# A GRU with a residual on one core: fewer warm-up products, one load moved, and the operand sums, banks and turns of the first steps rearranged

## The chip, the cores and the metric

The kernel runs on one core of a Trainium2 chip. Its metric is the device time in microseconds (us) of one execution; a lower time is better. Five engines work side by side, each on its own list of instructions in order, and they wait for each other by semaphores: TensorE (PE, matrix products, with the loading of weights shown apart as PEld), VectorE (DVE), ScalarE (ACT), GpSimd (POOL) and SyncE (SP, which here only issues transfers).

## What is computed

A recurrent unit runs over 128 steps for 64 sequences; both the input and the state h have 512 elements. The output is x plus all the new states.

```python
def step(h, inp):
    x_t, prop = inp
    comb = jnp.concatenate([x_t, h], axis=-1)
    z = jax.nn.sigmoid(comb @ Wz + bz)
    r = jax.nn.sigmoid(comb @ Wr + br)
    comb2 = jnp.concatenate([x_t, r * h], axis=-1)
    h_cand = jnp.tanh(comb2 @ Wh + bh)
    h_new = (1.0 - z) * h + z * h_cand
    h_next = jnp.where(prop, jnp.tanh(h_new @ Wp + bp), h_new)
    return (h_next, h_new)
```

`prop` is true in every fourth step but the last. All is in float32. Each weight has 1024 rows: the upper 512 multiply x, the lower 512 multiply h or r*h.

## The kernel before, in words

**Layout.** The 128 partitions hold two halves of the 512 columns for 64 sequences each, so that a state is a tile of 128 x 256. A product (`product`, L203, over `products`, L191) takes a 128-row block k of the transposed state as the stationary side and 256 columns of a weight as the moving side, once for each half. Each of these two matmuls is two records in the trace, so a product is four records and a gate, with its four blocks k, sixteen. The blocks are taken in the order 0, 2, 1, 3 (`ORDER`), and a weight arrives in two transfers, of blocks 0 and 1 and of blocks 2 and 3, so a gate's second product needs the second transfer.

**Turns.** Before h, r*h or x can be the stationary side, it is transposed: `turn` (L212) writes eight small transposes into PSUM, four into each of two banks (`turn_ps[c]`, c = 0 and 1), and DVE or ACT copies them out (L210). The sigmoid of r and the tanh of the candidate are written to another part of the same two banks (`act_ps`), from which DVE reads them.

**The step.** In the loop over t (L674) each step makes the products of r, then of z, the turn of r*h, and the products of the candidate; ACT and DVE make the gates and the new state (tanh L802, times z L803, plus the kept part L808); h is turned for the next step. The x part of each gate with its bias lies ready in `cp` and is copied into the gate's bank before the products (`seed`, L409, on ACT).

**The x part** is independent of the recurrence. Its products stand in a queue, and `fill(n)` (L417) puts n of them between the pieces of a step, so that PE has work while the other engines make the gates. Steps 0 to 3 and the last four use plain products (`plain`, L428). From step 4 on the steps are taken together in a scheme with seven products in place of eight, on two levels: the outer operands are numbered 1 to 7, and so are the inner ones (`batch`, L509, two outer products at a time). It needs sums of blocks of x, made on POOL (`sum_raw12`, `sum_raw34`, `sum_s12` and others), and sums of blocks of the x weights, made once at the start (`sum_outer`, and for each operand i `sum_inner(i, engine)`, three additions, and `sum_inner_1`, one in place). A batch uses four banks, `scratch` q, r, a and x, in which it makes first the products a, r, x, q and then x, q, r. After the first part ACT copies x and q out (L541, L542) and DVE adds (L543, L544, `end_1`); after the second ACT copies q (L549) and DVE adds r, x and q in this order (L550 to L552, `end_2`). Steps 4 to 7 use batches of their own: (1, 0) in step 1, (1, 1) and (1, 2) in step 2. POOL adds their results to the blocks in `cp` (`pair_left`, `pair_right`, L623 and L629).

**The start.** Transfers are issued on SP's queue in the order of the code, over eight semaphores, so that one waits for the landing of the one eight before it. PE makes products of zeros (`idle`, L179) and the turns of x of steps 0 and 1, then the x products of these two steps, the turn of h, and step 0. `turn_x(t)` turns the x of step t; ACT makes its copies from step 2 on. The x of steps 8 and later goes another way (`words_x`, `planes_x`, a transposing transfer, and `join_x`, on ACT).

The order on every engine is the order in which the code is written: nothing rearranges it.

Of the kernel before, what the change touches and what calls it, by code (L numbers as in the profile page):

```python
# [17 lines left out]
def kernel(  # L18
# [29 lines left out]
    nc = tc.nc  # L48
# [9 lines left out]
    FIRST = 2  # L58
    LAST = T // Q4 - 1
    R, Z, H_ = range(3)  # L60
# [74 lines left out]
    for i in range(3):  # L135
        for k in (0, 2):
            load_w(wh[i], gates_in[i][D:, :], k, k + 2, nc.sync)
        if i == 0:
            load_x(xr[0], 2, 2, 2)

    dummy = const.tile([1, 1], F32, name="dummy")
# [37 lines left out]
    def idle(n):  # L179
        for i in range(n):  # L180
            s = i % S
            nc.tensor.matmul(
                (rc, zp)[i // S % 2][s * B : (s + 1) * B, :, :],
                lhsT=zeros[:, :B],
                rhs=zeros,
                start=True,
                stop=True,
            )
# [14 lines left out]
    def product(ps, lT, w, k, start=False):  # L203
        s0, c0 = divmod(k, C)
        products(ps, lT[:, c0, ts(s0, B)], lambda s: w[:, k, ts(s, N)], start)
# [24 lines left out]
    def new_T(tag, name):  # L230
        return two.tile([P, C, P], F32, tag=tag, name=name)
# [7 lines left out]
    def new_xT(g):  # L239
        if g not in xT:  # L240
            xT[g] = xtp.tile([P, Q4, C, P], F32, tag="xT", name=f"xT_{g}")

    def turn_x(t, eng=nc.scalar):
        g, i = divmod(t, Q4)
        new_xT(g)
        src = xr[g] if g < 2 else early[g]
        for c in range(C):
            turn(src[:, i, :], xT[g][:, i], c, f"xT_{t}", eng)
# [79 lines left out]
    def sum_inner(i, eng):  # L328
        eng.tensor_sub(tt[:, i - 1, 1], inner(i, 1, 1), inner(i, 0, 1))
        eng.tensor_add(tt[:, i - 1, 0], tt[:, i - 1, 1], inner(i, 0, 0))  # L330
        eng.tensor_sub(tt[:, i - 1, 2], inner(i, 1, 0), tt[:, i - 1, 0])

    def sum_inner_1(i, eng):
        eng.tensor_sub(inner(i, 0, 1), inner(i, 0, 1), inner(i, 0, 0))  # L334
# [18 lines left out]
    def sum_raw34(g):  # L353
        v = xT[g]
        sx[g, 34] = one.tile([P, 4, C, B], F32, tag="s73", name=f"s34r_{g}")
        four([sx[g, 34][:, n] for n in range(4)], v[:, 2], v[:, 3])
# [6 lines left out]
    def sum_s12(g):  # L363
        v = xT[g]
        o = sx[g, "o12"] = one.tile([P, 2, 2, P], F32, tag="o12", name=f"o12_{g}")
        nc.gpsimd.tensor_add(o[:, 0], v[:, 2:4, 0, :], v[:, 2:4, 1, :])
        nc.gpsimd.tensor_sub(o[:, 1], o[:, 0], v[:, 0:2, 0, :])
        s = sx[g, 56] = one.tile([P, 4, 2, B], F32, tag="s56", name=f"s56_{g}")
        four([s[:, n] for n in range(4)], o[:, :, 0], o[:, :, 1])
# [47 lines left out]
    def fill(n):  # L417
        for _ in range(min(n, len(queue))):
            unit, end = queue.pop(0)
            unit()  # L420
            if end is not None:
                pending.append(end)
# [86 lines left out]
    def batch(n, ms):  # L509

        def region(ps, m):
            return ps[:, m].rearrange("p g u -> p (g u)")

        def unit(ps, m, j, e, start):
            g, i = ms[m]
            a, b = terms(i)[e]
            products(
                region(ps, m),
                lhs(g, a, j),
                lambda s: factor(b, j)[:, s],  # L520
                start and m == 0 and e == 0,
            )

        def units(ps, j, start):
            return [
                lambda m=m, e=e: unit(ps, m, j, e, start)
                for m, (_, i) in enumerate(ms)
                for e in range(len(terms(i)))
            ]

        def blocks():
            return MB[n].rearrange("p m b g (a u) -> p m b a g u", a=2)

        def end_1():
            MB[n] = mbp.tile([P, 2, 2, 3, P], F32, tag="mb", name=f"mb_{ms[0][0]}_{ms[0][1]}")
            for m, (g, i) in enumerate(ms):
                M[g, i] = MB[n][:, m]
            nm = len(ms)
            T2[n] = one.tile([P, 2, 3, P // 2], F32, tag="cx", name=f"cx_{ms[0][0]}_{ms[0][1]}")
            q1 = one.tile([P, 2, 3, P // 2], F32, tag="cq", name=f"cq_{ms[0][0]}_{ms[0][1]}")  # L540
            nc.scalar.copy(T2[n][:, :nm], x_ps[:, :nm])  # L541
            nc.scalar.copy(q1[:, :nm], q_ps[:, :nm])  # L542
            nc.vector.tensor_add(T2[n][:, :nm], r_ps[:, :nm], T2[n][:, :nm])  # L543
            nc.vector.tensor_add(blocks()[:, :nm, 0, 0], a_ps[:, :nm], q1[:, :nm])  # L544

        def end_2():
            q2 = one.tile([P, 2, 3, P // 2], F32, tag="cq", name=f"cq2_{ms[0][0]}_{ms[0][1]}")
            nm = len(ms)
            nc.scalar.copy(q2[:, :nm], q_ps[:, :nm])  # L549
            nc.vector.tensor_add(blocks()[:, :nm, 0, 1], r_ps[:, :nm], q2[:, :nm])  # L550
            nc.vector.tensor_add(blocks()[:, :nm, 1, 0], x_ps[:, :nm], q2[:, :nm])
            nc.vector.tensor_add(blocks()[:, :nm, 1, 1], q_ps[:, :nm], T2[n][:, :nm])  # L552

        free = units(a_ps, 2, True)
        one_ = [units(r_ps, 5, True), units(x_ps, 7, True), units(q_ps, 1, True)]

        one_ = sum(one_ if ms[0][0] >= FIRST else one_[2:] + one_[:2], [])
        two_ = units(x_ps, 4, False) + units(q_ps, 6, False) + units(r_ps, 3, False)
        seq = [(u, None) for u in free + one_ + two_]
        size = sum(len(terms(i)) for _, i in ms)  # L560
        for n_units, end in ((4 * size, end_1), (7 * size, end_2)):
            seq[n_units - 1] = (seq[n_units - 1][0], end)
        return seq
# [59 lines left out]
    def pair_left(a, p1, p2):  # L623
        nc.gpsimd.tensor_add(
            M[1, p2], M[1, p2], bias0.unsqueeze(1).to_broadcast([P, 2, 3, P])
        )
        add(c_block(1, a, 0), m_(1, p1), m_(1, p2))

    def pair_right(a, p1, x_):  # L629
        nc.gpsimd.tensor_add(  # L630
            M[1, x_], M[1, x_], bias[:, 1, 0:3, :].unsqueeze(1).to_broadcast([P, 2, 3, P])
        )
        add(c_block(1, a, 1), m_(1, p1), m_(1, x_))
# [11 lines left out]
    )  # L645


    idle(24)
    turn_x(0, nc.vector)
    idle(8)  # L650
    turn_x(1, nc.vector)
    idle(12)
    nc.gpsimd.tensor_sub(bias_d, bias[:, 1, 0:3, :], bias0)
    h = h_init
    hT = new_T("hT", "hT_init")
# [18 lines left out]
    for t in range(T):  # L674
# [3 lines left out]
        pair, u = divmod(t - 3, 8)  # L678
        even, odd = FIRST + 2 * pair, FIRST + 2 * pair + 1
        here = pair >= 0 and even * Q4 < T  # L680
        places = PLACES[u]
        if t == 0:
            queue.extend(plain(2) + plain(3))
            places = (12, 12)
        elif t == 1:
            queue.extend(batch((1, 0), [(1, 1), (1, 2)]))
            places = (8, 6)
        elif t == 2:
            queue.extend(batch((1, 1), [(1, 10), (1, 11)]) + batch((1, 2), [(1, 8), (1, 9)]))
            places = (12, 8)  # L690
        elif t == 3:
            queue.extend(batches(FIRST))
            places = (8, 8, 6)
# [3 lines left out]
        thin = t >= T - 9  # L697
        if thin:

            places, behind = TAIL[t - (T - 9)]  # L700
# [3 lines left out]
        if t == T - 10:  # L704

            places = (4, 6)
# [16 lines left out]
        for k in ORDER:  # L723
            product(slots[R], hT, wh[R], k)
        if t < 2:
            turn_x((2, 6)[t])
        if t == 1:
            for i in (7, 4):
                sum_inner(i, nc.gpsimd)
                sum_inner_1(i, nc.gpsimd)  # L730
        read_out()
        if t == 2:
            pair_left(0, 1, 2)
        if u == 0 and pair >= 1 and odd - 2 < LAST:
            outer_u2(odd - 2)
        if t == 3:
            sum_s12(FIRST)
        rh = two.tile([P, N], F32, tag="rh", name=f"rh_{t}")
        for c in range(C):
            nc.scalar.activation(act_ps[c], slots[R][:, ts(c, P)], AF.Sigmoid)  # L740
# [9 lines left out]

        for k in ORDER[: 2 if thin else 3]:
            product(slots[Z], hT, wh[Z], k)
        rhT = new_T("rhT", f"rhT_{t}")
        for c in range(C):
            turn(rh, rhT, c, f"rhT_{t}", nc.vector)
# [9 lines left out]
        nc.scalar.activation(slots[Z], slots[Z], AF.Sigmoid, scale=-1.0)  # L765
        nc.vector.tensor_mul(keep, slots[Z], h)
        join(1)
        if t == 1:
            sum_inner(5, nc.vector)
            sum_inner_1(5, nc.vector)  # L770
        seed(Z, t + 1)
        if prop:
            nc.scalar.copy(cut(slot_p), bias[:, :, 3, :])
# [40 lines left out]
            planes_x(3)  # L814
        read_out()
        fill(places[0] if thin else 5 if places[1] > 6 else 4)
        h = h_new
        if not last:
            hT = new_T("hT", f"hT_{t}")
            turn(h, hT, 0, f"hT_{t}", nc.vector)  # L820
            fill(places[1] if thin else 1 if places[1] > 6 else 2)
            turn(h, hT, 1, f"hT_{t}", nc.scalar)
        fill(places[2] if thin else places[1] - 6)
        if t == 0:
            sum_outer_1()
            for i in (1, 2, 3):
# [11 lines left out]
                turn(h, hT, c, f"hpT_{t}", (nc.vector, nc.scalar)[c])  # L838
            fill(behind[1] if thin else 2)
        if t == 0:  # L840
            turn_x(4)
            turn_x(5)
            sum_raw12(1)
        elif t == 1:
            turn_x(7)
            sum_raw34(1)
        elif t == 2:
            pair_right(0, 1, 10)
        elif t == 3:
            pair_left(1, 8, 9)  # L850
            pair_right(1, 8, 11)
# [35 lines left out]
                    outer_c12(odd)  # L887
        if u == 7 and pair >= -1 and (even + 2) * Q4 < T:
            sum_raw12(even + 2)
            if pair >= 0:  # L890
                sum_s12(even + 2)
        if pair >= 0:
            if u in (1, 2):
                for n in range(2):
# [11 lines left out]
        n = 0  # L906
        if t >= T - CHUNK:
            n = {T - 2: 3, T - 1: 1}.get(t, 0)
        elif j == Q4 - 1:
            n = 4  # L910
# [58 lines left out]
```

## Time and profile before

| | us |
|---|---|
| median of 3 runs | 1335.53 |
| lowest and highest | 1335.13 and 1337.05 |
| the profiled execution, its own time | 1334.71 |
| its span | 1332.9 |
| busy in it: PE, PEld | 1322.6, 1115.6 |
| busy in it: DVE, ACT, POOL | 706.6, 635.4, 932.5 |
| mean granted clock of PE | 0.999 |

An execution's own time is a little longer than the span of its trace. The costliest groups are the recurrent products, for instance

```profile
L194 PE MATMUL rc<-wh,rhT 128*64 128x256 f32 x2048 | 246.1, 379 | 0.0
L582 POOL TENSOR_TENSOR cp<-mb,mb 128x768 f32<-128x768 f32 x74 | 134.5, 1817 | 102.4 <-ACT rc L411 54.4
```

A group's line has the line of code, the engine, what is written from what, the number of instructions; then the busy time in us and the mean duration of one in ns; then how long the engine stood idle just before them, and what ended most of that. Matmuls overlap, so one lasts longer (379 ns) than the distance between two starts (0.108 us where sixteen take 1.73 us). In a timeline each row gives the start, the time until the last of the row's instructions ended, the instruction and, in brackets, the idle time before it with the releaser. A line of the waits gives the total, how often, and the longest.

### The profile page before, as it was taken

How to read it: one execution, taken by the hardware profiler on the slowest of the kernel's cores; microseconds unless marked ns; L12 is line 12 of the kernel's file. 1: busy time of each engine (PE TensorE's matmuls, PEld its weight loads, DVE VectorE, ACT ScalarE, POOL GpSimd, SP SyncE). 2: the span in 40 equal slices, each digit the busy share in tenths (PEclk: the TensorE clock that was granted, in tenths of full speed). 3: DMA queues.
4: the chain of work that ended last, by engine and by line, in shares of the span. 5: the costliest groups of instructions: out<-in, count | busy, mean ns of one | idle time of the engine just before them, and what ended most of it. 6: DMA issues, size and time to landing. Idle time of an engine off the chain costs nothing.

```text
span 1332.9 us, 37646 instructions
## 1 busy us (share of the span) xinstructions
PE 1322.6 (99%) x15336; PEld 1115.6 (84%) x15336; DVE 706.6 (53%) x1874; ACT 635.4 (48%) x1860; POOL 932.5 (70%) x1135
## 2 busy tenths in 40 slices
PE   9999999999999999999999999999999999999998
PEld 5788888888888888888888888888888888888765
DVE  3555555555555555555555555555555555555444
ACT  1454455454544544545445454445545444554433
POOL 5687876777777768776787767786777687767400
PEclk9999999999999999999999999999999999999999
DMA  9222233121221222313112221222212222131300
GB/s 293 45 49 49 49 65 64 33 65 39 59 65 33 65 51 47 65 40 81 42 40 58 64 65 33 56 43 65 65 33 65 49 50 65 33 76 38 98 24 17
DMA packets 119277, 77.79 MB, mean 58 GB/s; under 512 B 65984, under 2 KB 114240, under 8 KB 119104
## 3 DMA queue, kind: packets, MB, share of 16 engines
q1 hardware_dynamic: 118352, 74.14, 24.1%
q8 instruction: 121, 1.98, 0.6%
q10 hardware_dynamic: 496, 0.72, 0.2%
q0 software_dynamic: 256, 0.52, 0.1%
q14 instruction: 52, 0.43, 0.1%
HBM read 42.86 MB, written 16.78 MB: 45 GB/s over the span
## 4 chain that ended last, share of the span: by engine, by line
PE 96%; DMA 2%; DVE 1%; POOL 1%; ACT 0%; issue 0%; SPq 0%; DVEq 0%; ACTq 0%; POOLq 0%
PE rc L194 33%; PE zp L194 20%; PE scratch_q L194 11%; PE scratch_r L194 10%; PE scratch_x L194 10%; PE scratch_a L194 6%; PE turn L219 5%; DMA wh<-in_L_cond_Wz_dram 1%; DMA wx<-in_L_cond_Wz_dram 1%; POOL cp L582 0%; POOL mb L630 0%; ACT xT L283 0%; SPq L96 0%; DVE wx L334 0%; DVE tt L330 0%
## 5 line engine op out<-in xcount | busy, mean ns | idle before, releaser
L194 PE MATMUL rc<-wh,rhT 128*64 128x256 f32 x2048 | 246.1, 379 | 0.0
L582 POOL TENSOR_TENSOR cp<-mb,mb 128x768 f32<-128x768 f32 x74 | 134.5, 1817 | 102.4 <-ACT rc L411 54.4
L194 PE MATMUL zp<-wh,hT 128*64 128x256 f32 x1536 | 204.5, 379 | 0.0
L194 PEld LDWEIGHTS rc<-wh,rhT 128*64 128x64 f32 x2048 | 168.9, 137 | 39.9
L194 PE MATMUL rc<-wh,hT 128*64 128x256 f32 x1536 | 186.3, 383 | 0.3
L901 POOL TENSOR_TENSOR xr<-xr,h 128x256 f32<-128x256 f32 x127 | 92.7, 730 | 105.2 <-DVE h L808 105.2
L194 PEld LDWEIGHTS rc<-wh,hT 128*64 128x64 f32 x1536 | 121.6, 137 | 36.2 <-issue 9.8
L582 POOL TENSOR_TENSOR cp<-mb 128x768 f32<-128x768 f32 x46 | 83.6, 1816 | 95.1 <-ACT rc L411 93.7
L194 PEld LDWEIGHTS zp<-wh,hT 128*64 128x64 f32 x1536 | 119.3, 137 | 24.8
L210 DVE COPY rhT<-turn 128x256 uint16<-128x256 uint16 x256 | 97.5, 420 | 79.9 <-PE turn L219 78.8
L803 DVE TENSOR_TENSOR turn<-turn,z 128x128 f32<-128x128 f32 x256 | 75.4, 294 | 120.9 <-ACT turn L802 119.3
L740 ACT ACTIVATE turn<-rc 128x128 f32<-128x128 f32 x256 | 55.3, 260 | 167.3 <-issue 111.6
L210 ACT COPY hT<-turn 128x256 uint16<-128x256 uint16 x127 | 47.3, 373 | 168.6 <-DVE hT L210 130.4
L582 POOL TENSOR_TENSOR mb<-mb,mb 128x768 f32<-128x768 f32 x58 | 105.4, 1817 | 9.5 <-DVE mb L552 9.5
L411 ACT COPY rc<-cp 128x256 f32<-128x256 f32 x256 | 96.4, 376 | 25.9 <-DVE cp L436 14.4
L550 DVE TENSOR_TENSOR mb<-scratch_r,cq 128x384 f32<-128x384 f32 (+1 forms) x105 | 58.4, 556 | 93.2 <-ACT cq L549 93.2
L802 ACT ACTIVATE turn<-rc 128x128 f32<-128x128 f32 x256 | 55.2, 260 | 105.0 <-PE rc L194 103.9
L543 DVE TENSOR_TENSOR cx<-scratch_r,cx 128x384 f32<-128x384 f32 (+1 forms) x105 | 58.3, 556 | 86.2 <-ACT cx L541 86.2
L764 ACT ACTIVATE z<-zp 128x256 f32<-128x256 f32 x128 | 49.2, 384 | 96.2 <-PE zp L194 96.2
L283 ACT COPY xT<-xv 128x512 uint16<-128x512 uint16 x120 | 91.3, 764 | 0.0
L808 DVE TENSOR_TENSOR h<-turn,keep 128x128 f32<-128x128 f32 x254 | 74.0, 291 | 15.2
L219 PEld LDWEIGHTS <-h 128*64 128x64 bf16 x1016 | 68.3, 110 | 14.3 <-DVE h L808 7.9
(163 smaller groups left out, 3026.8 us busy)
## 6 DMA issues: line engine op xcount, KB each, us to landing
xr<-in_x_dram SPq DMA_DIRECT2D x62, 256.0 KB, 4.0
out_dram<-xr SPq DMA_DIRECT2D x62, 256.0 KB, 3.3
xs<-in_x_dram SPq DMA_DIRECT2D x56, 256.0 KB, 4.3
wx<-in_L_cond_Wz_dram SPq DMA_DIRECT2D x2, 512.0 KB, 8.0
wx<-in_L_cond_Wh_dram SPq DMA_DIRECT2D x2, 512.0 KB, 11.4
wh<-in_L_cond_Wr_dram SPq DMA_DIRECT2D x2, 512.0 KB, 13.4
wh<-in_L_cond_Wz_dram SPq DMA_DIRECT2D x2, 512.0 KB, 11.8
wh<-in_L_cond_Wh_dram SPq DMA_DIRECT2D x2, 512.0 KB, 10.9
```

The lines of the kernel that those rows point to most:

```text
L194: nc.tensor.matmul(ps[s * B : (s + 1) * B], lhsT=lhs, rhs=rhs(s), start=start, stop=True, skip_group_check=True,)
L210: (eng.copy if eng is nc.scalar else eng.tensor_copy)(dst, src)
L219: nc.tensor.transpose(pt[s * B : (s + 1) * B, w, :], words.rearrange("p (n w) -> p w n", w=2)[:, w, :], ident16,)
L283: nc.scalar.copy(xT[g][:, i].bitcast(U16).rearrange("p c (n w) -> p w c n", w=2), xv[g][:, i])
L411: nc.scalar.copy(cut(slots[i]), G[t][:, :, i, :])
L543: nc.vector.tensor_add(T2[n][:, :nm], r_ps[:, :nm], T2[n][:, :nm])
L550: nc.vector.tensor_add(blocks()[:, :nm, 0, 1], r_ps[:, :nm], q2[:, :nm])
L582: nc.gpsimd.tensor_add(dst, a, b)
L740: nc.scalar.activation(act_ps[c], slots[R][:, ts(c, P)], AF.Sigmoid)
L803: nc.vector.tensor_mul(pc, pc, z[:, ts(c, P)])
L808: nc.vector.tensor_add(h_new[:, ts(c, P)], pc, keep[:, ts(c, P)])
L901: nc.gpsimd.tensor_add(xr[g][:, j, :], xr[g][:, j, :], h_new)
```

## The change

The change touches only the start and steps 0 to 3.

- 44 products of zeros become 28: 16 before the turn of x of step 0, 4 before that of step 1, 8 after it.
- The x of steps 2 and 3 is loaded behind the recurrent weights of z instead of in front of them.
- The turn of x of step 2 goes from behind r's products of step 0 to behind the first three of z's.
- The turn of x of step 4 goes from the end of step 0 to the middle of the last six x products there; that of step 5 stays at the end.
- The turn of x of step 7, and the sums of x of steps 6 and 7, go from the end of step 1 to in front of h's turn.
- The sums of operand 5 go from DVE to POOL, in front of those of operand 7; those of operand 4 go from step 1 to step 2.
- The batch (1, 2) makes its products in the order a, r, x, q, as the later ones do; (1, 0) and (1, 1) keep a, q, r, x.
- On POOL `pair_right(0, 1, 10)` goes behind the sums of x of steps 8 to 11, and the second set of these sums from step 3 to the end of step 2.

```diff
-        if i == 0:
+        if i == Z:
             load_x(xr[0], 2, 2, 2)
...
-        one_ = sum(one_ if ms[0][0] >= FIRST else one_[2:] + one_[:2], [])
+        one_ = sum(one_[2:] + one_[:2] if n in ((1, 0), (1, 1)) else one_, [])
...
-    idle(24)
+    idle(16)
     turn_x(0, nc.vector)
+    idle(4)
+    turn_x(1, nc.vector)
     idle(8)
-    turn_x(1, nc.vector)
-    idle(12)
...
         if t < 2:
-            turn_x((2, 6)[t])
+            if t:
+                turn_x(6)
         if t == 1:
-            for i in (7, 4):
+            for i in (5, 7):
                 sum_inner(i, nc.gpsimd)
                 sum_inner_1(i, nc.gpsimd)
         read_out()
         if t == 2:
             pair_left(0, 1, 2)
+            sum_inner(4, nc.gpsimd)
+            sum_inner_1(4, nc.gpsimd)
...
-        if t == 3:
-            sum_s12(FIRST)
...
         for k in ORDER[: 2 if thin else 3]:
             product(slots[Z], hT, wh[Z], k)
+        if t == 0:
+            turn_x(2)
         rhT = new_T("rhT", f"rhT_{t}")
...
-        if t == 1:
-            sum_inner(5, nc.vector)
-            sum_inner_1(5, nc.vector)
...
         fill(places[0] if thin else 5 if places[1] > 6 else 4)
+        if t == 1:
+            turn_x(7)
+            sum_raw34(1)
         h = h_new
         if not last:
             hT = new_T("hT", f"hT_{t}")
             turn(h, hT, 0, f"hT_{t}", nc.vector)
             fill(places[1] if thin else 1 if places[1] > 6 else 2)
             turn(h, hT, 1, f"hT_{t}", nc.scalar)
-        fill(places[2] if thin else places[1] - 6)
+        if t == 0:
+            fill(3)
+            turn_x(4)
+            fill(3)
+        else:
+            fill(places[2] if thin else places[1] - 6)
...
         if t == 0:
-            turn_x(4)
             turn_x(5)
             sum_raw12(1)
-        elif t == 1:
-            turn_x(7)
-            sum_raw34(1)
-        elif t == 2:
-            pair_right(0, 1, 10)
...
             sum_raw12(even + 2)
-            if pair >= 0:
-                sum_s12(even + 2)
+            sum_s12(even + 2)
+        if t == 2:
+            pair_right(0, 1, 10)
```

## The prediction

> **What bounds the kernel now.** I read the profile page first, for the engine that carries the span. In these lines of it the reader is to see that TensorE (PE) is busy 99% of the span and that the chain that ended last lies 96% on it, so an edit pays only where it removes time in which PE stands still, or work from PE itself.
>
> ```profile
> PE 1322.6 (99%) x15336; PEld 1115.6 (84%) x15336; DVE 706.6 (53%) x1874; ACT 635.4 (48%) x1860; POOL 932.5 (70%) x1135
> PE 96%; DMA 2%; DVE 1%; POOL 1%; ACT 0%; issue 0%; SPq 0%; DVEq 0%; ACTq 0%; POOLq 0%
> ```
>
> Next, the waits of PE over the first 130 us. The whole run adds hardly any (its largest sum, 1.6, is the 1.4 below and one more), so all that waits can still give is 3.6 us, and the wait for the first zeros, which the change leaves.
>
> ```profile
> PE turn L219 <- DVE h L808: 1.4, 1, 1.4
> PE rc L182 <- DVE zeros L73: 1.2, 1, 1.2
> PE zp L194 <- DMA wh<-in_L_cond_Wz_dram: 0.7, 1, 0.7
> PE scratch_q L194 <- DVE mb L552: 0.5, 1, 0.5
> PE turn L219 <- ACT hT L210: 0.4, 1, 0.4
> PE turn L219 <- ACT xT L210: 0.4, 1, 0.4
> PE scratch_r L194 <- POOL s L344: 0.2, 1, 0.2
> ```
>
> Third, PE's timeline of the start (first column: start, us). The reader is to see two rates, 0.43 us for two zero products up to 7.17 and 0.21 after it, then x products without a gap, and at 23.41 the wait for the second half of z's recurrent weights.
>
> ```profile
> 6.75 0.62 PE L182 MATMUL rc<-zeros 128*64 128x512 bf16 x2
> 7.17 0.40 PE L182 MATMUL zp<-zeros 128*64 128x512 bf16 x2
> 7.42 0.38 PE L182 MATMUL rc<-zeros 128*64 128x512 bf16 x2
> ...
> 9.37 1.89 PE L194 MATMUL scratch_q<-wx,xT 128*64 128x256 f32 x16
> ...
> 23.41 1.08 PE L194 MATMUL zp<-wh,hT_init 128*64 128x256 f32 x8 [0.69 <-DMA wh<-in_L_cond_Wz_dram]
> 24.32 0.39 PE L219 MATMUL turn<-ident,rh 128*64 128x128 bf16 x8
> 24.55 0.60 PE L194 MATMUL zp<-wh,hT_init 128*64 128x256 f32 x4
> ```
>
> Last, VectorE (DVE) in step 1: the four sums of operand 5 hold it from 43.95 to 48.25, and h, done at 49.79, comes after them.
>
> ```profile
> 43.95 0.55 DVE L329 TENSOR_TENSOR tt<-wx 128x384 f32<-128x384 f32 x1
> 44.53 1.24 DVE L330 TENSOR_TENSOR tt<-tt,wx 128x384 f32<-128x384 f32 x1
> 45.80 1.25 DVE L331 TENSOR_TENSOR tt<-wx,tt 128x384 f32<-128x384 f32 x1
> 46.97 1.36 DVE L334 TENSOR_TENSOR wx<-wx 128x384 f32<-128x384 f32 x1
> 48.25 0.54 DVE L543 TENSOR_TENSOR cx<-scratch_r,cx 128x384 f32<-128x384 f32 x1
> ```
>
> I sum against the profiled execution: span 1332.9, its own time 1334.71, which is 0.82 under the median of the runs, 1335.53. A measurement of this kernel tells about 0.2% (2.7 us) from no change.
>
> **Fewer zeros.** 44 zero products become 28: 16 x 0.21 = 3.4 us at the slow rate. With two turns at 0.43 each, PE is done with them at 1.20 + 3.42 + 0.43 + 0.85 + 0.43 = 6.33, plus eight zeros across the change of rate, 7.6, instead of 9.37. But then the weights rule. The trace's landings (the last of a transfer's 16 parts): x weights of r 7.88, of z 9.20 and 12.16, of h 14.50 and 15.83; recurrent r 17.67 and 19.78; x of steps 2 and 3 20.50 and 20.89; recurrent z 22.03 and 23.37. A product takes 0.43, and the second product of each gate needs the second half. So, after the change: first product 7.92; z's second waits for 12.16; the recurrent r's second, ready at 19.34, waits for 19.78; all of r is done at 21.1.
>
> Here a rule speaks against the cut. The row: the rate doubles at 7.2, 6.0 us after PE's first product. The Trainium skill ("TensorE: Matmul & The Clock Gate", What's actually happening) says that the clock is doubled only after a busy window of about 3.4 us, and that the windows run free of the kernel. To be sure to hold one whole window, PE must be busy for two, 6.83 us. The cut leaves 28 x 0.2135 + 2 x 0.43 = 6.84 at the slow rate, from 1.20 to 8.04: just enough. By the row nothing is lost, by the rule's worst phase 0.1 us; I take nothing. The opposite fear, that the new pauses for weights halve the clock again, has a row too: between 48.2 and 51.6 PE stands still for 1.35 + 0.36 us, and the gate that starts at 51.50 still takes 1.73 us.
>
> **x of steps 2 and 3 behind z's weights.** These two transfers take 20.89 - 19.78 = 1.11 us of the stream. Without them in front, z's halves land at 20.9 and 22.26, and x at 22.98 and 23.37, the same total. On SyncE's queue the four transfers swap places: z's go out at 6.43 and 7.89, x at 9.56 and 12.17, over ten us before it lands, so the issue is not late. PE: first z product at 21.1, second waits to 22.30, two products to 23.16. There the turn of x of step 2 now stands, and waits for 23.37: 23.42. The turn of r*h behind it writes the same two banks, so it waits for ScalarE's (ACT) copies out of them. The trace has this pair: two turns one after the other at 37.52 took 1.14 us until the next product instead of 0.44. So the last z product comes at 23.42 + 1.14 = 24.56, as before 24.55. ACT has room (1.80 us idle before z). I take +0.1; bounds -0.5 (x lands with z) and +0.5 (x 0.4 later). The zeros are hidden by the same landing: with all 44, PE would have reached z's second product at 22.50.
>
> **Turns of steps 4 and 5 apart.** That same pair, 1.14 us before step 1, is split: the first goes between six x products (0.43 each, three after), so its copies end before the second. 0.44 remain: -0.70. Bounds -0.75 and -0.5. The in-place sums behind it on DVE come 0.2 later and end at about 40.1, 0.7 before they would hold up r*h.
>
> **Operand 5's sums to GpSimd (POOL), step 1's turn of step 7 ahead of h's.** DVE is free, so (in the clock of before) the first copies end at 46.92 and 47.31 on ACT, L543 runs at 47.0, L544 at 47.45, then h's halves end at 48.51 and 49.04. The changed program's instruction order shows that the turn of step 7 waits for DVE, which reads the same banks until h is done: its halves come at 48.57 and 49.10. h's first turn waits for ACT's copy of step 7, which starts 0.33 after the first transpose and takes 0.37: 49.33. Then 0.11, two r units 0.65, 0.11: step 2 starts at 50.20 instead of 51.50, -1.30. Bounds: -1.7 (both stalls wholly gone, 1.35 + 0.36) and -0.9 (each of the four handovers 0.1 longer).
>
> POOL pays with time that is covered. One operand's four sums take 4 x 1.05 = 4.2 there (L329 to L329, 15.99 to 19.12 for three). Operand 5 is done at 46.0, 7 at 50.2, the sums of steps 6 and 7 at 51.9; PE wants the latter at 55.2. Operand 4 moves behind step 1's additions to xr and to the left blocks, ends at 60.5, and is first needed several batches later. If this cover were gone, PE would wait for the rest one for one.
>
> **The order of step 2.** The third batch of step 2 waited 0.74 us start to start (66.65 to 67.39) as its q bank is read last by DVE. Taking r first starts at 66.65, since r is read by 66.4 and x by 66.9. But then h's turn, at 67.62, meets h, which ends at 67.93: 67.98, one unit, the other half at 68.53, two units, step 3 at 69.29 instead of 69.62: -0.3, not -0.74. Bounds -0.5 and -0.1.
>
> **pair_right behind the sums of steps 8 to 11.** Those sums (5.1 us) start when ACT has joined xT, 63.1, and end at 68.2; pair_right's two additions (3.7) end at 71.9. ACT's seed of step 4, 70.5 in this clock, waits for that, and behind it on ACT the copy of q (L549), 1.5 late at 72.8; DVE wants it at 74.0, after r*h. Covered by 1.2. The wait at 76.28 stays: there DVE's L550 stands behind r*h's copies, in both kernels. From step 4 on nothing differs.
>
> **Sum.** +0.1 - 0.7 - 1.3 - 0.3 = -2.2: 1332.5 for the profiled execution, and with 0.82 a median of 1333.3, -0.17%.
>
> **Rivals.** (a) The start gains too. If transfers run faster than in this profile, before is held by its PE work (gapless from 9.37, only 0.69 behind the weights) and after by the weights: -0.5 to -1.4 more, 1331.9 to 1332.8. For it: 0.69 is little; against: 332 to 350 GB/s in this stretch, all engines full. 25%. (b) The change does less than it says: x lands 0.5 late and the new handovers in shared banks take back half of step 1: -0.8 to -1.5, 1334.0 to 1334.7. 10%. (c) Slower, by the clock alone: the cut of the zeros leaves no whole busy window in an unlucky phase, and pauses then break each later one. Half rate costs half of the PE time that it covers; the pauses for weights hide 0.4 + 0.5 + 0.7 = 1.6 of that, and 2.2 is gained elsewhere. To lose 2.7, half rate must last 13 us, to about 21; to 24.6 it costs some 7: 1340. Against it stands the kept rate at 51.50. 4%. The likeliest case has 61%.
>
> **How the numbers follow.** The likeliest case by itself runs from 1332.7 to 1333.9, by the bounds of step 1 and x's landing. Eight in ten: from the middle of (a) less 0.7 for the runs' own scatter (1335.13 to 1337.05) to the end of (b) and as much, 1331.6 to 1335.2. Faster by over 0.2% means under 1332.86: all of (a) and a ninth of the likeliest, 32%. Slower: (c) and a bad draw, 5%. Within: 63%.
>
> **What would show it.** Right: the first x product at 7.9; a PE wait of about 0.75 for z's weights near 22.3 and of 0.25 for x near 23.4; r*h's turn waiting for ACT's xT; step 1 starting 0.6 earlier, step 2 1.9, step 3 2.2 earlier; waits of PE for h of 0.3 at step 2's end. Wrong: z's last start product clearly before 24.1 or after 25.0, zero products at 0.21 instead of 0.11 or gates at 3.5 instead of 1.73 after 8.1, or a PE wait for POOL between 50 and 75.

## The result and the profile after

| | before | after |
|---|---|---|
| median of 20 runs each, us | 1335.75 (1335.06 to 1337.48) | 1333.75 (1332.85 to 1335.46) |
| profiled execution: own time, span | 1334.71, 1332.9 | 1334.15, 1332.3 |

The ratio is 0.9985, with a 95% interval of 0.9979 to 0.9991: 2.0 us faster, 0.15%. The forecast was 1333.3, within 0.2%. The two profiled executions differ by only 0.56 us, because that of before lay 1.04 under its median and that of after 0.40 above. So the shares below are taken from differences inside one trace, and only then set against the medians.

The engine line and the chain of the page say the same as before: TensorE carries the span.

```profile
PE 1321.7 (99%) x15320; PEld 1110.8 (83%) x15320; DVE 702.6 (53%) x1870; ACT 635.4 (48%) x1860; POOL 934.9 (70%) x1139
PE 96%; DMA 2%; DVE 1%; ACT 1%; issue 0%; SPq 0%; DVEq 0%; ACTq 0%
```

PE's waits in the first 130 us (the columns are the sum in us, the number of waits, the longest):

```profile
PE zp L194 <- DMA wh<-in_L_cond_Wz_dram: 1.4, 2, 1.1
...
PE turn L219 <- DVE h L808: 0.4, 2, 0.2
...
PE turn L219 <- ACT xT L210: 0.3, 1, 0.3
...
PE scratch_r L194 <- DVE mb L550: 0.2, 1, 0.2
PE turn L219 <- DMA xr<-in_x_dram: 0.2, 1, 0.2
```

The wait of 1.4 for h is now 0.4 in two pieces, the waits for DVE's read of the q bank (0.5) and for hT (0.4) are gone, and the weights of z cost 1.4 instead of 0.7. The wait of 0.2 for POOL's sums in before is the one for L550 here: it stands ahead of the same product of step 3 (76.28 in before, 75.65 in after, 0.22 both times), and only the releaser that the list names has changed. In after POOL's sums are done at 68.9, so this wait is not for them.

PE's timeline of the start (the first column is the start in us):

```profile
7.82 1.95 PE L194 MATMUL scratch_q<-wx,xT 128*64 128x256 f32 x16 [0.36 <-DMA wx<-in_L_cond_Wr_dram]
...
23.73 1.08 PE L194 MATMUL zp<-wh,hT_init 128*64 128x256 f32 x8 [1.13 <-DMA wh<-in_L_cond_Wz_dram]
24.98 0.42 PE L219 MATMUL turn<-ident,xr 128*64 128x128 bf16 x8 [0.17 <-DMA xr<-in_x_dram]
25.75 0.58 PE L219 MATMUL turn<-ident,rh 128*64 128x128 bf16 x8 [0.35 <-ACT xT L210]
26.13 0.63 PE L194 MATMUL zp<-wh,hT_init 128*64 128x256 f32 x4
```

The cut of the zeros brings the first x product from 9.37 to 7.82, and nothing of that is left at the end: the last start product is at 26.13, where before had 24.55. The reason is in the trace's landings: the last of the 16 parts of x arrived at 24.85, not at the 23.37 that the sum took over from before. The other 15 parts were there at 23.25.

The end of step 1 on VectorE, and then on PE:

```profile
47.85 0.56 DVE L543 TENSOR_TENSOR cx<-scratch_r,cx 128x384 f32<-128x384 f32 x1 [2.93 <-ACT cx L541]
...
49.65 0.29 DVE L808 TENSOR_TENSOR h<-turn,keep 128x128 f32<-128x128 f32 x1
```

```profile
49.46 0.31 PE L219 MATMUL turn<-ident,xr 128*64 128x128 bf16 x4
49.99 0.31 PE L219 MATMUL turn<-ident,xr 128*64 128x128 bf16 x4 [0.22 <-DVE h L808]
50.23 0.31 PE L219 MATMUL turn<-ident,h 128*64 128x128 bf16 x4
50.34 0.85 PE L194 MATMUL scratch_r<-wx,s12r 128*64 128x192 f32 x8
50.99 0.31 PE L219 MATMUL turn<-ident,h 128*64 128x128 bf16 x4
51.12 1.95 PE L194 MATMUL rc<-wh,hT 128*64 128x256 f32 x16
```

VectorE stood idle for 2.93 us ahead of L543; operand 5's sums, which held it until 48.25, are gone. h ends at 49.94, 10.4 after the start of step 1 (39.55); in before it was 11.1 (38.66 to 49.79). PE goes through the turn of step 7 with one short wait.

Measured from mark to mark, the two traces compare so. "Landing" is the last part of the last transfer that the start waits for: z's weights in before, x in after. The steps are taken at the first product of their r gate.

| stretch, us | before | after | after, a second profile | predicted (with a sign: the change) |
|---|---|---|---|---|
| last landing | 23.37 | 24.85 | 23.87 | 23.37 |
| landing to last start product | 1.18 | 1.28 | 1.29 | 1.19 |
| last start product to step 1 | 14.11 | 13.42 | 13.42 | -0.70 |
| step 1 to step 2 | 12.84 | 11.57 | 11.57 | -1.30 |
| step 2 to step 3 | 18.12 | 17.86 | 17.85 | -0.3 |
| step 3 to step 5 | 25.37 | 25.37 | 25.37 | 0 |

All but the first row repeat within 0.01. The profiled execution sums to +1.48 + 0.10 - 0.69 - 1.27 - 0.26 = -0.64, and its span is 0.6 shorter. The three terms after the start give -2.22; the medians differ by -2.0, which leaves +0.2 for a typical start. The interval of the ratio alone lets that be anything from -0.6 to +1.0.

### The profile page after: what moved, and what is told of

Its sections match the earlier page's. It is cut to its first block, busy times and chain, and to the rows that moved or that the text cites. A ratio compares the mean times of both kernels' runs of the same rounds, so it can differ in the third digit from the quotient of the medians.

```text
span 1332.3 us, 37617 instructions
## 1 busy us (share of the span) xinstructions
PE 1321.7 (99%) x15320; PEld 1110.8 (83%) x15320; DVE 702.6 (53%) x1870; ACT 635.4 (48%) x1860; POOL 934.9 (70%) x1139
## 4 chain that ended last, share of the span: by engine, by line
PE 96%; DMA 2%; DVE 1%; ACT 1%; issue 0%; SPq 0%; DVEq 0%; ACTq 0%
PE rc L194 33%; PE zp L194 20%; PE scratch_q L194 11%; PE scratch_r L194 10%; PE scratch_x L194 10%; PE scratch_a L194 6%; PE turn L219 5%; DMA xr<-in_x_dram 1%; DMA wx<-in_L_cond_Wz_dram 1%; ACT xw L210 0%; ACT xT L283 0%; DVE h L808 0%; DVE turn L803 0%; SPq L96 0%; DVE mb L550 0%
## 5 line engine op out<-in xcount | busy, mean ns | idle before, releaser
L411 ACT COPY rc<-cp 128x256 f32<-128x256 f32 x256 | 96.4, 377 | 26.7 <-DVE cp L436 13.6
L550 DVE TENSOR_TENSOR mb<-scratch_r,cq 128x384 f32<-128x384 f32 (+1 forms) x105 | 58.3, 555 | 92.7 <-ACT cq L549 92.7
L543 DVE TENSOR_TENSOR cx<-scratch_r,cx 128x384 f32<-128x384 f32 (+1 forms) x105 | 58.3, 556 | 88.8 <-ACT cx L541 88.8
```

What stands on the lines that cost most here:

```text
L411: nc.scalar.copy(cut(slots[i]), G[t][:, :, i, :])
```

## The experiments

Two theories. The first is the prediction's: three terms of -0.7, -1.3 and -0.3, each from one rearrangement, and a start that gives nothing. The rivals: the start gains or loses by itself (landings, clock), and the handovers in shared banks, not the work that was moved, set the size of each term. Two groups of four kernels and one of three ran, each group on one chip with the kernel before beside it: 1335.66, 1335.72 and 1335.64 us there. Where no diff is shown, the description is the whole edit.

**again.** The kernel after, once more, for a second profile.

> The changed kernel once more, for its landings. Theory (the late start of the first trace is that execution's landings, not the change): x of steps 2 and 3 lands between 23 and 24 instead of 24.85, the last start product comes 1.2 to 1.3 us after it, and from that product step 1 begins 13.4 later, step 2 25.0, step 3 42.9, as in the first trace, within 0.15. Rival (the new order of the loads itself delays x): x lands near 24.8 again.

1333.18 in one run. Its profile is the fourth column of the table above: with x landed at 23.87, step 3 starts at 68.00 against 69.62 in before. The landing is what moves between executions; the rest stands.

**zeros_only.** The kernel before with the after's zeros:

```diff
-    idle(24)
+    idle(16)
     turn_x(0, nc.vector)
-    idle(8)
+    idle(4)
     turn_x(1, nc.vector)
-    idle(12)
+    idle(8)
```

> The kernel before with 28 zero products instead of 44, nothing else. Theory (the start waits for the recurrent weights of z): first x product near 7.9 instead of 9.37, the wait for z's second half about 1.4 us longer in all, the last start product 1.2 after that half's landing as before; time within 0.5 us of before. Rival (the zeros are worth what they take): 1.4 to 3.4 us faster.

1335.38, ratio 0.9999 [0.9990, 1.0008]. The first x product comes at 7.79 instead of 9.37, and the last start product 1.18 after z's landing (23.70), as in before. The cut by itself is worth nothing: the weights' landing sets that product, with 44 zeros or with 28.

**start_only.** zeros_only, and the load and the turn of step 2 moved as in after:

```diff
-        if i == 0:
+        if i == Z:
             load_x(xr[0], 2, 2, 2)
...
         if t < 2:
-            turn_x((2, 6)[t])
+            if t:
+                turn_x(6)
...
             product(slots[Z], hT, wh[Z], k)
+        if t == 0:
+            turn_x(2)
```

> The kernel before with the zeros cut, x loaded behind z's weights and the turn of x of step 2 behind z's first three products, nothing else. Theory: the last start product 1.2 to 1.3 after the landing of x instead of 1.2 after that of z's second half, so within 0.3 us of before (my +0.1); no later stall goes. Rival (the start is where the gain comes from): 0.7 to 1.5 us faster.

1336.11, ratio 1.0005 [0.9996, 1.0013]: 0.45 above before in its group, where at most 0.3 was expected, and 0.73 above zeros_only, with intervals that overlap. In its profile x landed at 25.64, 2.3 later than its other 15 parts, and the last start product came 1.29 behind it. Between that mark and step 1, and in each later step, it has the times of before within 0.02.

**few_zeros.** The kernel after with four zeros instead of 28, then the two turns. The four stay because they also open the banks' accumulation.

```diff
-    idle(16)
+    idle(4)
     turn_x(0, nc.vector)
-    idle(4)
     turn_x(1, nc.vector)
-    idle(8)
```

> The changed kernel with 4 zero products instead of 28. Theory (a clock not yet granted costs only what the waits for weights don't hide): zeros and turns end by about 5.5, the first gate begins at 7.9 at half rate (3.5 us a gate), the rate doubles [...]near 10 to 14, so 1 to 3 us of work are lost of which 1.5 are hidden: 0 to 1.5 us slower than the changed kernel. Rival (the waits keep the clock at half until the start is over): 5 to 8 us slower.

1333.92, ratio 0.9988 [0.9979, 0.9997], against 0.9985 for after: no difference that can be told. Its timeline of PE at the start:

```profile
7.78 3.68 PE L194 MATMUL scratch_q<-wx,xT 128*64 128x256 f32 x16 [1.46 <-DMA wx<-in_L_cond_Wr_dram]
11.25 3.16 PE L194 MATMUL scratch_a<-wx,xT 128*64 128x256 f32 x16
14.25 1.89 PE L194 MATMUL scratch_q<-wx,xT 128*64 128x256 f32 x16
```

The first gate takes 3.47 us from start to start instead of 1.73. The rate doubles only at 13.81, 6.0 us after 7.78, and stays. Until then PE does its products at half rate, where at full rate it would have waited for the weights: in after it waits 0.5 for z's x weights, 0.3 for the recurrent ones of r and 1.4 for those of z, and here none of these waits is left. The last start product comes at 25.54, 1.47 after x's landing, against 1.28: PE's own products, without a gap from 7.78 to 24.40, set it there, 0.2 later than the landing would have.

**sums_only.** The kernel before with operand 5's sums on POOL ahead of operand 7's, and operand 4's in step 2:

```diff
-            for i in (7, 4):
+            for i in (5, 7):
...
             pair_left(0, 1, 2)
+            sum_inner(4, nc.gpsimd)
+            sum_inner_1(4, nc.gpsimd)
...
-        if t == 1:
-            sum_inner(5, nc.vector)
-            sum_inner_1(5, nc.vector)
```

> The kernel before with the sums of operand 5 on GpSimd in front of those of 7 and those of 4 in step 2, nothing else; the turn of step 7 and its sums stay where they were. Counted from step 1's start, step 2 began 12.84 later in the kernel before and 11.57 in the changed one. Theory (the stall was DVE's alone): h's first turn 0.1 after h, about 48.6 in the clock of before, then the 1.65 us that followed it before: step 2 begins 11.5 to 11.6 after step 1, so the turn's move gives nothing. Rival (the move of the turn is needed for the 0.36 us wait for ACT): 11.9 to 12.0.

1333.85 in one run; step 1 to step 2 takes 11.56, where after has 11.57. PE's timeline:

```profile
48.67 0.31 PE L219 MATMUL turn<-ident,h 128*64 128x128 bf16 x4
48.81 0.82 PE L194 MATMUL scratch_r<-wx,s12r 128*64 128x192 f32 x8
49.47 0.28 PE L219 MATMUL turn<-ident,h 128*64 128x128 bf16 x4
49.58 0.28 PE L219 MATMUL turn<-ident,xr 128*64 128x128 bf16 x4
50.22 0.31 PE L219 MATMUL turn<-ident,xr 128*64 128x128 bf16 x4 [0.36 <-ACT hT L210]
```

The turn of step 7 stands behind h's as in before, and between its halves loses 0.64 - 0.11 = 0.53 to ACT's copy of hT, with 0.23 more ahead of 48.67. In after it stands ahead of h's turn and loses as much, 0.23 before 49.46, 0.42 before 49.99 and 0.13 before 50.23. The whole of the term is the sums' move.

**sums_turn7.** sums_only, and the turn of step 7 (with the sums of steps 6 and 7 behind it) ahead of h's turn, as in after.

> The same, and the turn of step 7 with its sums moved in front of h's turn. Theory: step 2 begins 11.57 after step 1, as in the changed kernel, since its turn waits for DVE and h's turn for ACT's copy. Rival: 0.3 or more earlier than in the run with the sums alone.

1334.35 in one run, in which the landing was at 24.04 instead of 23.47 (sums_only). Step 1 to step 2: 11.57. The turn's move gives nothing on its own, though it takes away the wait for hT.

**split_order.** The kernel before with the turn of step 4 between the x products of step 0, and the new order of the batch (1, 2) in step 2:

```diff
-        fill(places[2] if thin else places[1] - 6)
+        if t == 0:
+            fill(3)
+            turn_x(4)
+            fill(3)
+        else:
+            fill(places[2] if thin else places[1] - 6)
...
-            turn_x(4)
             turn_x(5)
...
-        one_ = sum(one_ if ms[0][0] >= FIRST else one_[2:] + one_[:2], [])
+        one_ = sum(one_[2:] + one_[:2] if n in ((1, 0), (1, 1)) else one_, [])
```

> The kernel before with the turn of step 4 among the x products and with the third batch of steps 4 to 7 in the order a, r, x, q, nothing else. Theory: from the last start product step 1 begins 13.42 later instead of 14.11, step 2 12.84 after step 1 as before, step 3 17.85 after step 2 instead of 18.12. Rival for the order (the bank was the whole wait): 17.4.

1334.99 in one run, with z's weights landed at 24.51. Last start product to step 1 is 13.42 (before 14.11): -0.69. Step 1 to step 2 is 12.83, as in before. Step 2 to step 3 is 17.81 (before 18.12): -0.31. Both terms come from these edits alone, and since they lie in different steps, each can be told from the other.

**own_banks.** The kernel after with other banks for two turns: that of step 2 writes the two scratch banks that are free then, that of step 7 z's bank, so that neither waits for the banks of r*h and h.

```diff
-        pt = turn_ps[c][:, :P].bitcast(BF16)
+        pt = (turn_ps[c][:, :P] if bank is None else bank).bitcast(BF16)
...
+            bank = {2: scratch[2 + c][:, :P], 7: slot_p[:, ts(c, P)]}.get(t)
```

> The changed kernel, but the turn of x of step 2 is written into the banks scratch a and x, and that of step 7 into the spare half of z's bank, instead of the two banks of the turns. Theory (two new waits come from these shared banks: 0.7 at r*h's turn in step 0, 0.75 at h's turn in step 1): last start product 0.5 to 0.6 after x's landing instead of 1.28, step 2 10.8 to 10.9 after step 1 instead of 11.57; 1.4 us faster than the changed kernel, near 1332.3. Rival (the waits are for ACT's and DVE's work, whatever the bank): as the changed kernel.

1333.17, ratio 0.9979 [0.9970, 0.9988]: 0.6 under after, not the 1.4 that was expected. The start went as the handover theory had it: last start product 0.58 after x's landing instead of 1.28. Step 1 to step 2 fell only to 11.40. Its timeline shows why:

```profile
48.32 0.28 PE L219 MATMUL zp<-ident,xr 128*64 128x128 bf16 x4
49.07 0.31 PE L219 MATMUL zp<-ident,xr 128*64 128x128 bf16 x4 [0.47 <-ACT xT L210]
49.18 0.31 PE L219 MATMUL turn<-ident,h 128*64 128x128 bf16 x4
```

The first half is free at once (48.32), but the second lies in the same bank, in other columns, and PE starts it only when ACT has copied the first. The wait moved from h's banks to the turn's own. Whether the chip or the program's own semaphores make the second half wait was not tried.

**load_front.** The kernel after with the load of x back in front of z's weights.

> The kernel after, with one line put back: the load of x of steps 2 and 3 stands again in front of z's recurrent weights, while the turn of step 2 stays behind z's three products. Theory A (the handover in the shared banks prices the place of the turn): the last start product comes 0.87 (two products) + 1.14 (two turns in the same banks) = 2.0 us after the last landing of z's weights, against 1.28 after x's landing in the kernel after; for landings that end at the same time that is 0.7 slower, 1334.4 where the kernel after has 1333.7. Theory B (the new order of the loads makes the last part land later by about 0.5 to 1 us): the time is that of the kernel after or up to 0.3 below it, and the last part lands near 23.5.

1333.67, ratio 0.9985 [0.9976, 0.9994]: the time of after, as theory B had it, though the handover of theory A is in the profile: last start product 2.10 after the landing (24.56), of which 0.36 is the wait for ACT's copy. Theory B's landing near 23.5 is not in this profile, but it is that of the slowest of the eleven runs (1334.68). A costlier handover and an order of loads that lands earlier would cancel so; one profile doesn't prove it.

**no_start.** The kernel after with load and turn of step 2 where before has them; the cut of the zeros stays.

> The kernel after without its start: load and turn of step 2 where the kernel before has them; the cut of the zeros, the turns of steps 4 and 5 apart, the sums of operand 5, the turn of step 7 and the order of step 2 stay. Theory A (the start edits are worth +0.1, as predicted, and landings alone scatter): last start product 1.2 after z's last landing, the three other terms -0.69 -1.27 -0.27 unchanged, median 1333.5 to 1333.8, the same as the kernel after. Theory B (the start edits cost 0.5, by a later last part): median about 1333.2. Theory C (they gain): over 1334.

1333.43, ratio 0.9981 [0.9972, 0.9990]. Landing to last start product is 1.19, and the later stretches are 13.42, 11.55 and 17.85. It lies 0.3 under after, between theories A and B, with intervals that overlap.

**best.** own_banks, with two further edits: the first half of the turn of step 7 stands directly behind h's products, ahead of the x products that follow, and in step 3 the additions that read the batches stand ahead of r*h's turn, so that VectorE reads before it copies.

```diff
+        if t == 1:
+            turn_x(7, halves=[0])
         fill(places[0] if thin else 5 if places[1] > 6 else 4)
         if t == 1:
-            turn_x(7)
+            turn_x(7, halves=[1])
...
+        if t == 3:
+            read_out()
         rhT = new_T("rhT", f"rhT_{t}")
...
-        if t in (2, 3):
+        if t == 2:
             read_out()
```

> The kernel with its own banks for the two turns, where the first half of the turn of step 7 goes into z's bank directly behind h's products of step 1, ahead of the four x products, and the second half stays behind them; and in step 3 the additions that read the batches stand ahead of the copies of r*h on VectorE. Theory A (the shared bank of the two halves was all that was left in step 1): no wait for ScalarE's xT near 49, step 1 to step 2 10.75 to 10.85 instead of 11.40, no wait near 74.5 and 0.3 to 0.4 less in step 3; median 1333.2 - 0.6 - 0.4 = 1332.2. Theory B (h is next: its second half ends too late for the second turn): 11.0 to 11.2 for the step, median 1332.5 to 1332.8.

1332.09 (median of 6 runs), ratio 0.9972 [0.9960, 0.9983]: theory A, and faster than both kernels. PE's timeline of the end of step 1:

```profile
47.10 0.28 PE L219 MATMUL zp<-ident,xr 128*64 128x128 bf16 x4
...
48.57 0.31 PE L219 MATMUL zp<-ident,xr 128*64 128x128 bf16 x4
48.68 0.31 PE L219 MATMUL turn<-ident,h 128*64 128x128 bf16 x4
48.79 0.85 PE L194 MATMUL scratch_r<-wx,s12r 128*64 128x192 f32 x8
49.44 0.31 PE L219 MATMUL turn<-ident,h 128*64 128x128 bf16 x4
49.55 1.93 PE L194 MATMUL rc<-wh,hT 128*64 128x256 f32 x16
```

No wait is left in these rows. Step 1 to step 2 takes 10.82, -0.58 against own_banks, and step 3 to step 5 24.95, -0.42: the 0.2 that the profile put down to DVE's L550 was 0.4 between products. The two further edits lie in different steps, so each stretch tells of one.

## Why the prediction was right, point by point

**Bound.** Right in kind: only time in which PE stood still could be had, and the three terms are such time. But 3.6 us is not all that those waits can give. The list counts a wait from the end of the row ahead, and rows overlap: a turn's row lasts 0.39 us, where the next product can start after 0.22. So the two turns at 37.52 lost 0.53 between their starts (0.75 for 0.22), with 0.36 listed. In step 1 the list has 1.35 + 0.36, from which the text took its bound of -1.7, and best took 2.02 out there (12.84 to 10.82).

**Fewer zeros.** Right: nothing (zeros_only). The sum's first product, 7.92, came at 7.82. The clock rule did no harm, as the row had it. The Trainium skill ("TensorE: Matmul & The Clock Gate", What's actually happening) wants a busy window of about 3.4 us with windows that run free. By an estimate from that figure, as the text's 6.83 us is one, the change of rate would come 3.4 to 6.8 us after PE's first product. In the twelve profiles with 28 or more zeros, all with that product at 1.20, it came 2.7 to 6.0 us after it. Two lie below the estimate, 2.7 (sums_only) and 3.1 (no_start), so for these the rule, as applied here, does not hold, and the measurement stands; none lies above it.

Rival (c) let half rate cost half of the PE time under it, less 1.6 us of pauses for the weights. few_zeros ran at half rate from 7.78 to 13.81, 6.0 us: by that sum 3.0 - 1.6 = 1.4 lost. It lost 0.2, since there were more pauses to fill: its work from 7.78 to the turn at 24.40 takes 16.62, so 13.6 at full rate, and after needs 17.16 for the same work (7.82 to 24.98). That is 3.5 us of pauses, 0.8 of them by after's later landing. Half rate to 21, as the rival had it, was not seen in any run.

**x behind z's weights.** The step that failed. The handover was right: 1.28 after the landing for 1.19, with the 0.35 for ACT's copy that the sum named, and own_banks shows that it is the bank's (0.58 without it). What failed is the term "x at 22.98 and 23.37, the same total": in the two profiles of after x was complete at 24.85 and 23.87, and the wait for z's weights, put at 0.75 near 22.3, was 0.28 and 1.13 in the first (at 21.95 and 23.73). By the text's own test (wrong, if the last start product comes after 25.0) this step was wrong in both, 26.13 and 25.16. The marks for "right" in the clock of before, step 1 0.6, step 2 1.9 and step 3 2.2 earlier, were not met either: step 1 came 0.89 later, step 2 0.38 and step 3 0.64 earlier, and in the second profile 0.08, 1.35 and 1.62 earlier.

The 22.50 for z's second product with all 44 zeros still holds the wait for z's first half, which the new order takes away; without it PE is there at 22.11. The landing hides the zeros either way.

All profiles together:

| order of the loads | whole last landing, us | 15 of its 16 parts | lag of the 16th part at the last landing | lag at the second half of r's recurrent weights |
|---|---|---|---|---|
| z's weights last (7 kernels) | 23.37, 23.47, 23.70, 23.71, 24.04, 24.51, 24.56 | 22.71 to 23.92 | 0.66, 0.39, 0.14, 0.20, 0.12, 1.08, 1.59 | 0.80, 0.73, 0.28, 0.01, 0.35, 1.20, 1.62 |
| x last (6 kernels) | 23.87, 24.07, 24.64, 24.73, 24.85, 25.64 | 23.25 to 23.82 | 0.14, 0.48, 0.96, 0.91, 1.60, 2.27 | 0.22, 0.14, 0.40, 0.80, 1.26, 1.85 |

The lag is the time by which the last part lands behind the 15th; the lists of a row have the profiles in the same order. The 23.37 that the sum took over from before is the earliest landing of all thirteen. The 15 parts arrive at much the same time in both orders; the last part lags by 0.1 to 2.3 us, by a median of 0.4 in the first order and 0.9 in the second. Most of that lag is older than the swap. The second half of r's recurrent weights is loaded ahead of the swapped transfers in both orders, and where its last part lagged by over 1 us (four profiles, two of each order), the last landing lagged by 1.1 to 2.3. Of the 1.48 by which after's first profile landed later than before's, 0.54 is the 15 parts (22.71 to 23.25) and 0.94 the lag (0.66 to 1.60), and of its lag of 1.60 the swapped transfers had 1.26 from ahead of them.

What the new order may add is smaller: from the one transfer to the other the lag changed by -0.34 to +0.19 with z's weights last (median -0.14) and by -0.08 to +0.56 with x last (median +0.34). That is some 0.5 us, read afterwards from thirteen single executions, with ranges that overlap. The times of the runs allow for it and don't prove it: the start costs +0.2 by the sum of terms, +0.3 by no_start, +0.7 by start_only against zeros_only, where the forecast had +0.1 with bounds of -0.5 and +0.5; none of the three is clear of its noise. The gain of 0.5 to 1.4 that rival (a) wanted is in none of them. Of (b), the part that has x late by 0.5 happened, and the part that takes back half of step 1 did not. Why one part lags stays open.

**Turns of steps 4 and 5 apart.** Right: -0.69 for -0.70, three times over (after, again, split_order).

**Operand 5's sums, turn of step 7.** Right in size and, to a few hundredths, in place: moved to the clock of before (step 1 at 38.66, so 0.89 earlier), the turn of step 7 stands at 48.57 and 49.10, h's at 49.34, step 2 at 50.23; the text had 48.57, 49.10, 49.33 and 50.20. But the heading credited two edits, and one does it all: sums_only has the whole -1.28, and the turn's move changed 0.01: it exchanges the wait for hT for gaps ahead of h. That 0.75 was left to be had there, best shows (10.82 for 11.57). The bound of -1.7 was too narrow, as said under Bound. POOL's cover held: operand 5 was done at 47.0, operand 4 at 61.5, and no wait of PE in the first 130 us is for POOL.

**Order of step 2.** Right: -0.26 for -0.3. h's first turn (67.66) then starts 0.35 later than the products ahead of it would let it, 0.18 of that listed as a wait; the text had 67.98 for 67.62, 0.36. That wait is why the 0.74 did not come.

**pair_right.** Right: nothing lost, step 3 to step 5 is 25.37 in both. ACT's seed did wait for POOL, 1.17 us until 72.57, as the text had it; the copy of q behind it ended at 73.35, and DVE read it at 74.95. The wait that the sum left standing behind r*h's copies stood, and best took it out: its cause, the order on VectorE, is shown.

**Sum.** -2.2 predicted, -2.0 by the medians: the three terms came in at -2.22 for -2.3, and the difference is the start, +0.2 for +0.1. The rest of the gap between 1333.3 and 1333.75 is the reference: the profile of before lay 1.04 under the median of 20 runs, not 0.82. For the three terms the sum is earned, each with its mechanism. For the start the agreement is luck: x landed 1.5 and 0.5 later than the +0.1 had it in the two profiles of after, and the times cannot tell +0.1 from +0.7. (The upper end of the range, 1335.2, is 0.2 below what its own words give, 1334.7 + 0.7.)

## What to carry to other kernels

A stall at a shared buffer is taken out by asking who reads the buffer last, down to which half: a turn that moved ahead of h's gained nothing until its two halves had a free bank and time between them. Where a stretch is set by a landing, work taken out of PE ahead of it gives nothing, and a load moved to the end of the queue makes the last part of that load the bound. A list of waits is a lower figure: what a stall costs is read from start to start (0.53 for 0.36, 0.42 for 0.22 here). A profile shows stretches between marks to some 0.02 us and a start that scatters by 2: compare the stretches, and leave the start to many runs.

## What was not expected of the hardware

PE at half rate until 13.81 us cost 0.2 us by the profile and nothing that the times can tell (1333.92 against 1333.75). And the last transfer that the start waits for was complete only 0.1 to 2.3 us behind its 15th part, while the 15th itself came between 22.71 and 23.92 in all 13 profiles. The lag is carried from one transfer to the next: in load_front the last part was 2.15 behind the 15th at the first half of r's recurrent weights, and still 1.59 at the last landing, five transfers later. Last, the rate of PE's products doubled anywhere from 2.7 to 6.0 us after the first one, in kernels that begin alike.
